# One instruction per head for the causal mask and the row maximum of the attention scores

## The chip, the cores and the metric

The kernel runs on one core of a Trainium2 chip. The metric is the device time of one execution in microseconds (us); less is better. A core has five engines with a queue of instructions each: TensorE (PE, matrix products; its weight loads are shown as PEld), VectorE (DVE), ScalarE (ACT), GpSimd (POOL) and SyncE (SP, which here only issues DMA transfers). An engine takes its instructions strictly in the order in which they were written, and waits on semaphores for the results of others. SBUF is the on-chip memory with 128 partitions; PSUM is the memory that TensorE writes to.

## The reference

Four sequences of 512 tokens with 1024 features go through causal attention with 32 heads (8 key and value heads, 32 features each), and then through a linear layer with a two-of-eight choice of low-rank additions. All is float32. What the change touches is this:

```python
scores = jnp.einsum('bhqd,bhkd->bhqk', q, k) / math.sqrt(HEAD_DIM)
scores = jnp.where(causal[None, None, :, :], scores, jnp.float32(-1e+20))
attn = jax.nn.softmax(scores, axis=-1)
out = jnp.einsum('bhqk,bhkd->bhqd', attn, v)
...
result = jnp.einsum('bsd,od->bso', x, base_w) + base_b
```

Around it stand layer norms, the projections for queries, keys and values, rotary embedding, the output projection, and the gate with its low-rank products.

## The kernel before

**Tiles.** The 2048 tokens are 16 tiles of 128 (`Tokens`, line 854). Tile `t` is number `i = t % 4` of its sequence, so that its queries meet `n = (i + 1) * 128` keys. The projections work on pairs of tiles in seven products of half blocks each, in place of eight (`seven`, line 724). Their bias is added when a product leaves PSUM: the lower half of the bias with the first product, and for the fourth the "bias step", which is the upper half less the lower half (`bias_step`, line 461; `bias_steps`, line 414). All four projections ("kv", "q", "o" and "f", the last one with `bbase_sb`) have a tile of their own for the step.

**Attention in groups.** The heads of a tile are done in groups (`Group`, line 1479). A group takes `n` heads of each of four quadrants (32 partitions each): 4 for `i` = 0, 2 for `i` = 1 and one for `i` = 2 and 3. That makes 2, 4, 8 and 8 groups for the four tiles of a sequence, 88 in all. `scores` (line 1490) has TensorE write the scores of all four quadrants into the only score tile `sc`, four PSUM banks, one for each quadrant. Then `softmax` (line 1552) runs on DVE in two parts of two quadrants each: line 1567 adds the triangular mask `cmask` to the last 128 columns of each row of scores, in place, and line 1577 takes the maximum of each whole row, negated, into `nmax`. For each quadrant, ACT computes exp(score + nmax) into `pr` and sums it (line 1519; with each goes a second instruction that reads the accumulator out), DVE takes the reciprocal of the sums (line 1548), and POOL multiplies (line 1533). TensorE transposes `pr` (line 1670), ACT or DVE copies the result out of PSUM (line 336 or 337, `prT<-pt_p`), and TensorE multiplies it with the values (line 1693). The next group's scores need the score tile free, that is all of this group's exponentials done.

**What sets the order.** No run-time scheduler: `Order` (line 92) plans the whole kernel when it is built. Every step on DVE, ACT, POOL and SP has a cost in us written into the code, and a rank ("urgent"; lower goes first); a step that may run on either of two engines, such as `copy` (line 332) and `combine` (line 340), goes to the one that is free sooner by these costs. TensorE's steps lie in lanes; the planner takes a step that is ready by its own clock, attention first and the dense projections into the gaps, and then prints all queues in that order. So a changed cost moves instructions in every queue. On the chip each queue keeps the printed order, whether or not the costs were right. The matmuls that use TensorE in parts of 32 rows or columns (scores and values) are planned next to each other, where that is possible (`PAIRED`, line 254); a step counts as safely ready when its inputs are `SAFE` = 0.3 us old by the plan (line 223).

Of the kernel before, what the change touches and what calls it, by code (L numbers as in the profile page):

```python
# [11 lines left out]
F32 = mybir.dt.float32  # L12
AF = mybir.ActivationFunctionType
ALU = mybir.AluOpType
AX = mybir.AxisListType

P = 128
# [5 lines left out]
MASKED = -1e30  # L23
QUADS = P // HD
# [67 lines left out]
class Order:  # L92
# [10 lines left out]
    def start(self, chain, at=0.0):  # L103
        task = Task()
        self._go_on(chain, task, at)
        return task
# [159 lines left out]
def kernel(  # L266
# [14 lines left out]
    nc = tc.nc  # L281
    NT, D = x.shape
    S = rope.shape[0]
# [12 lines left out]
    const = ctx.enter_context(tc.tile_pool(name="const", bufs=1))  # L296
# [20 lines left out]
    order = Order(banks)  # L317
    start = order.start

    def dve(us, urgent, issue):  # L320
        return Op(urgent, dve=(us, issue))

    def act(us, urgent, issue):
        return Op(urgent, act=(us, issue))

    def pool(us, urgent, issue):
        return Op(urgent, pool=(us, issue))
# [12 lines left out]
    def combine(urgent, out, in0, in1, op, engines=("dve", "pool"), n=512):  # L340
# [11 lines left out]

    ident = const.tile([P, P], F32, name="ident")
    make_identity(nc, ident)
    cmask = const.tile([P, P], F32, name="cmask")
    make_causal_mask(nc, cmask, MASKED)

    earlier = const.tile([P, E, E], F32, name="earlier")
# [2 lines left out]
        out=earlier,  # L361
# [15 lines left out]
    bbase_sb = const.tile([P, D], F32, name="bbase_sb")  # L377
# [9 lines left out]
    def loads(what):  # L387
# [13 lines left out]
    plain = {"kv": w_qkv[:, D:], "q": w_qkv[:, :D], "o": w_o, "f": w_base}  # L401

    width = {name: 256 if name == "kv" else 512 for name in plain}
# [8 lines left out]
        "f": bbase_sb,  # L412
    }
    bias_steps = {
        name: const.tile([P, width[name]], F32, name=f"bias_step_{name}") for name in plain
    }
    has_bias = {name: Task() for name in plain}

    def new_wide(name):
# [1070 lines left out]
    def scores(g):  # L1490

        tok, seq = g.tok, g.seq
        i, n = tok.i, (tok.i + 1) * P
        sc = ps_sc.tile([P, QUADS, 512], F32, tag="sc", name=f"sc_{g.name}")
        for c in range(g.n):
            for r in range(QUADS):
                rows = slice(r * HD, (r + 1) * HD)
                nc.tensor.matmul(  # L1498
                    sc[:, r, c * n : (c + 1) * n],
                    lhsT=tok.qT[g.kt][rows, (g.at + c) % GROUP, :],  # L1500
                    rhs=seq.kT[g.kt][rows, :n],
                    start=True,
                    stop=True,
                )
        sc4 = sc[:, :, : g.n * n].rearrange("p r (c k) -> p r c k", c=g.n)
        nmax = small.tile([P, QUADS, GROUP], F32, tag="nmax", bufs=3, name=f"nmax_{g.name}")
        total = small.tile([P, QUADS, GROUP], F32, tag="total", bufs=3, name=f"total_{g.name}")
        rtot = small.tile([P, QUADS, GROUP], F32, tag="rtot", bufs=3, name=f"rtot_{g.name}")

        def quadrant(r):  # L1510
            urgent = 1 + r / QUADS
            yield soft_slots.take()
            pr = soft.tile([P, GROUP, P], F32, tag="soft", name=f"pr_{g.name}_{r}")
            pr = g.pr[r] = pr.rearrange("p a b -> p (a b)")
            for c in range(g.n):
                yield act(
                    0.5 + n * 0.00079,
                    urgent,
                    lambda: nc.scalar.activation(  # L1519
                        pr[:, c * n : (c + 1) * n],  # L1520
                        sc4[:, r, c, :],
                        AF.Exp,
                        bias=nmax[:, r, c : c + 1],
                        accum_out=total[:, r, c : c + 1],
                    ),
                )
            g.exps[r].finish(order.at)
            yield g.rtot[r // 2]
            for c in range(g.n):
                yield pool(  # L1530
                    0.33 + n * 0.00089,
                    urgent,
                    lambda: nc.gpsimd.tensor_scalar(  # L1533
                        pr[:, c * n : (c + 1) * n],
                        pr[:, c * n : (c + 1) * n],
                        rtot[:, r, c : c + 1],
                        1.0,
                        ALU.mult,
                        ALU.mult,
                    ),  # L1540
                )
            g.normed[r].finish(order.at)

        def totals(h):
            some = slice(2 * h, 2 * h + 2)
            yield g.exps[some]
            yield dve(
                0.18, 1, lambda: nc.vector.reciprocal(rtot[:, some, : g.n], total[:, some, : g.n])  # L1548
            )
            g.rtot[h].finish(order.at)  # L1550

        def softmax():
            yield g.scored.done
            tok.q_left[g.kt] -= g.n
            if not tok.q_left[g.kt]:
                qT_slots.give(order.at)
            seq.left[g.kt] -= g.n
            if not seq.left[g.kt]:
                kT_slots.give(order.at)
            q = QUADS // g.parts  # L1560
            for r0 in range(0, QUADS, q):
                some = slice(r0, r0 + q)
                diag = sc4[:, some, :, i * P : n]
                yield dve(
                    0.15 + q * g.n * 0.135,
                    0,
                    lambda: nc.vector.tensor_tensor(  # L1567
                        out=diag,
                        in0=diag,
                        in1=cmask.unsqueeze(1).unsqueeze(1).to_broadcast([P, q, g.n, P]),  # L1570
                        op=ALU.add,
                    ),
                )
                yield dve(
                    0.15 + q * g.n * n * 0.00105,
                    0,
                    lambda: nc.vector.tensor_reduce(  # L1577
                        nmax[:, some, : g.n], sc4[:, some], AX.X, ALU.max, negate=True
                    ),
                )  # L1580
                for r in range(r0, r0 + q):
                    start(quadrant(r), order.at)

        start(softmax(), order.now)
        for h in range(QUADS // 2):
            start(totals(h), order.now)
# [192 lines left out]
    for tok in line:  # L1779
        n = min(GROUP, NQ // (tok.i + 1))  # L1780
# [5 lines left out]
    for k, g in enumerate(groups):  # L1786
# [6 lines left out]
        if k > 1:  # L1793
            needs += [s.done for s in groups[k - 2].turned]
        g.scored = Step(0.218 * blocks, partial(scores, g), needs, soon=soon)
        if tok.squares:
            g.scored.tiled = True
# [191 lines left out]
```

## Time and profile before

| what | value |
| --- | --- |
| time, median of 3 runs | 1162.27 us (1158.39 to 1164.69) |
| time of the profiled execution | 1156.95 us |
| its span, from first to last instruction | 1155.2 us |
| DVE busy | 842.5 us, 73% |
| ACT busy | 527.2 us, 46% |
| POOL busy | 636.6 us, 55% |
| DMA, bytes moved | 251.05 MB, mean 217 GB/s |
| granted TensorE clock over the span | 0.997 |

The rows of the profile read `line engine operation out<-in partitions x elements xcount | busy us, mean ns of one | idle time before, and who ended it`. A line is that of the kernel above, and of a helper where a helper issues the instruction. Busy time is a union, so that overlapping instructions are counted once. The time of an execution is about 1.75 us more than its span.

### The profile page before, as it was taken

How to read it: one execution, taken by the hardware profiler on the slowest of the kernel's cores; microseconds unless marked ns; L12 is line 12 of the kernel's file. 1: busy time of each engine (PE TensorE's matmuls, PEld its weight loads, DVE VectorE, ACT ScalarE, POOL GpSimd, SP SyncE). 2: the span in 40 equal slices, each digit the busy share in tenths (PEclk: the TensorE clock that was granted, in tenths of full speed). 3: DMA queues.
4: the chain of work that ended last, by engine and by line, in shares of the span. 5: the costliest groups of instructions: out<-in, count | busy, mean ns of one | idle time of the engine just before them, and what ended most of it. 6: DMA issues, size and time to landing. Idle time of an engine off the chain costs nothing.

```text
span 1155.2 us, 22058 instructions
## 1 busy us (share of the span) xinstructions
PE 1125.2 (97%) x7464; PEld 637.7 (55%) x7464; DVE 842.5 (73%) x1661; ACT 527.2 (46%) x1542; POOL 636.6 (55%) x875
## 2 busy tenths in 40 slices
PE   7999899999999999999999999999999999999997
PEld 3455555655446556665466455656754555556543
DVE  4778867878778876788778676688866787657564
ACT  0345555455435544465354245456453555454010
POOL 3676867763756644545665356464635564547231
PEclk9999999999999999999999999999999999999999
DMA  9777668656797458546696656754657744586682
GB/s 342 276 273 267 226 211 278 232 191 223 258 334 236 134 181 260 182 146 201 223 290 195 227 175 219 234 168 152 196 173 261 226 138 154 166 268 194 216 288 79
DMA packets 136239, 251.05 MB, mean 217 GB/s; under 512 B 14912, under 2 KB 30912, under 8 KB 136128
## 3 DMA queue, kind: packets, MB, share of 16 engines
q1 hardware_dynamic: 136128, 249.65, 65.3%
q8 instruction: 60, 0.98, 0.4%
q14 instruction: 51, 0.42, 0.1%
HBM read 225.87 MB, written 23.07 MB: 215 GB/s over the span
## 4 chain that ended last, share of the span: by engine, by line
PE 86%; DVE 7%; DMA 2%; POOL 2%; ACT 2%; issue 1%; SPq 0%; POOLq 0%; ACTq 0%; DVEq 0%
PE acc_f L646 19%; PE acc_o L646 16%; PE acc_q L646 13%; PE pt_p L1670 11%; PE acc_kv L646 8%; PE sc L1498 7%; PE av L1693 6%; PE acc_gl L646 2%; DVE nmax L1577 2%; PE pt_h L621 1%; PE pt_q L1121 1%; PE pt_xn L621 1%; ACT pr L1519 1%; POOL pr L1533 1%; DMA xa<-in_x_dram 1%
## 5 line engine op out<-in xcount | busy, mean ns | idle before, releaser
L1533 POOL TENSOR_SCALAR pr<-pr,rtot 128x256 f32<-128x256 f32 (+3 forms) x512 | 309.9, 620 | 220.6 <-DVE rtot L1548 158.2
L1519 ACT ACTIVATE pr<-sc,nmax 128x256 f32<-128x256 f32 (+3 forms) x512 | 264.1, 536 | 107.1 <-DVE nmax L1577 58.0
L1577 DVE TENSOR_REDUCE nmax<-sc 128x2 f32<-128x768 f32 (+3 forms) x176 | 198.2, 1126 | 32.0 <-ACT pr L1519 28.6
L336 ACT COPY prT<-pt_p 128x512 f32<-128x512 f32 (+1 forms) x260 | 132.8, 546 | 86.9 <-PE pt_p L1670 86.1
L1670 PE MATMUL pt_p<-ident,pr 128*128 128x128 f32 x1216 | 165.8, 276 | 2.2 <-DVE raw_k L1026 0.8
L1670 PEld LDWEIGHTS pt_p<-ident,pr 128*128 128x128 f32 x1216 | 137.9, 142 | 53.7 <-issue 39.9
L336 ACT COPY aT<-av 128x128 f32<-128x128 f32 (+2 forms) x82 | 25.1, 306 | 220.7 <-PE av L1693 202.0
L1567 DVE TENSOR_TENSOR sc<-sc,cmask 128x256 f32<-128x256 f32 (+2 forms) x176 | 96.5, 548 | 39.4 <-PE sc L1498 34.0
L646 PE MATMUL acc_f<-piece,s_f 128*128 128x512 f32 x256 | 118.7, 595 | 2.1 <-DVE s_f L344 2.1
L1519 ACT ACTIVATION_READ_ACCUMULATOR pr<-sc,nmax 128x1 f32 x512 | 109.0, 213 | 0.0
L646 PE MATMUL acc_o<-piece,aT 128*128 128x512 f32 x232 | 106.1, 594 | 0.0
L646 PE MATMUL acc_q<-piece,T_xn 128*128 128x512 f32 x224 | 105.2, 594 | 0.0
L646 PE MATMUL acc_o<-piece,s_o 128*128 128x512 f32 x224 | 103.2, 594 | 1.1 <-DMA piece<-in_w_qkv_dram 1.1
L1498 PE MATMUL sc<-kT,qT 32*128 32x384 f32 (+3 forms) x1024 | 94.3, 465 | 1.3 <-ACT pr L1519 1.3
L646 PE MATMUL acc_f<-piece,T_h 128*128 128x512 f32 x192 | 89.9, 594 | 0.1
L1693 PEld LDWEIGHTS av<-prT,v 128*32 128x32 f32 x2432 | 61.7, 109 | 49.0 <-issue 34.7
L344 POOL TENSOR_TENSOR y<-y,w 128x512 f32<-128x512 f32 x61 | 78.1, 1298 | 16.1 <-DVE w L590 8.6
L1693 PE MATMUL av<-prT,v 128*32 128x128 f32 x2432 | 84.9, 276 | 0.5 <-ACT T_xn L336 0.2
L646 PE MATMUL acc_kv<-piece,T_xn 128*128 128x512 f32 (+1 forms) x224 | 84.3, 511 | 0.8 <-DMA piece<-in_w_qkv_dram 0.8
L569 POOL TENSOR_TENSOR rstd<-veps,neg_half 128x1 f32<-128x1 f32 x64 | 36.3, 571 | 77.8 <-DVE veps L565 70.4
L646 PE MATMUL acc_q<-piece,s_q 128*128 128x512 f32 x160 | 75.2, 593 | 0.0
L646 PEld LDWEIGHTS acc_f<-piece,s_f 128*128 128x128 f32 x256 | 46.5, 190 | 51.8 <-issue 42.5
(178 smaller groups left out, 1544.9 us busy)
## 6 DMA issues: line engine op xcount, KB each, us to landing
piece<-in_w_qkv_dram SPq DMA_DIRECT2D x132, 256.0 KB, 3.8
piece<-mixed_f SPq DMA_DIRECT2D x128, 256.0 KB, 3.4
piece<-in_w_o_dram SPq DMA_DIRECT2D x116, 256.0 KB, 3.3
piece<-mixed_q SPq DMA_DIRECT2D x112, 256.0 KB, 3.5
piece<-mixed_o SPq DMA_DIRECT2D x112, 256.0 KB, 4.2
piece<-in_w_base_dram SPq DMA_DIRECT2D x96, 256.0 KB, 3.5
xa<-in_x_dram SPq DMA_DIRECT2D x32, 256.0 KB, 3.6
y<-in_x_dram SPq DMA_DIRECT2D x16, 512.0 KB, 5.2
```

What stands on the lines that cost most here:

```text
L336: act=(0.15 + n * 0.00085, lambda: nc.scalar.copy(out(), in_())),
L344: engine.tensor_tensor(out=out(), in0=in0(), in1=in1(), op=op)
L569: nc.gpsimd.tensor_tensor(out=self.rstd, in0=self.veps, in1=neg_half, op=ALU.pow)
L621: nc.tensor.transpose(pt[:, c, :], src()[:, at : at + P], ident)
L646: nc.tensor.matmul(acc[0][:, :n], lhsT=lhsT(c), rhs=w(c), start=(c == 0), stop=last)
L1498: nc.tensor.matmul(sc[:, r, c * n : (c + 1) * n], lhsT=tok.qT[g.kt][rows, (g.at + c) % GROUP, :], rhs=seq.kT[g.kt][rows, :n], start=True, ...
L1519: lambda: nc.scalar.activation(pr[:, c * n : (c + 1) * n], sc4[:, r, c, :], AF.Exp, bias=nmax[:, r, c : c + 1], accum_out=total[:, r, c : ...
L1533: lambda: nc.gpsimd.tensor_scalar(pr[:, c * n : (c + 1) * n], pr[:, c * n : (c + 1) * n], rtot[:, r, c : c + 1], 1.0, ALU.mult, ALU.mult,),
L1567: lambda: nc.vector.tensor_tensor(out=diag, in0=diag, in1=cmask.unsqueeze(1).unsqueeze(1).to_broadcast([P, q, g.n, P]), op=ALU.add,),
L1577: lambda: nc.vector.tensor_reduce(nmax[:, some, : g.n], sc4[:, some], AX.X, ALU.max, negate=True),
L1670: nc.tensor.transpose(pt[:, j, :], g.pr[r][:, j * P : (j + 1) * P], ident)
L1693: nc.tensor.matmul(av[r * HD : (r + 1) * HD, c, :], lhsT=g.seq.v[j][:, head * HD : (head + 1) * HD], rhs=g.prT[r][:, c * (i + 1) + j, :], ...
```

## The change

A wider mask tile holds 384 columns of zeros ahead of the triangle, so that its last `n` columns are the mask of a whole row of scores. For tiles with `i` > 0, the mask addition and the maximum become one DVE instruction for each head and quadrant, `tensor_tensor_reduce`: it writes -(score + mask) over the scores, and their minimum, which is the negated maximum, to `nmax`. ACT then computes exp(-x + nmax). The quadrants start in order, each when its own rows are done. Tiles with `i` = 0 keep the two instructions. The planner is given 0.17 + 0.00105 n us for the new instruction, without a term for the read of the accumulator.

The bias step of "f" is no longer a tile of its own: it is written over the upper half of `bbase_sb`, which nothing else reads.

```diff
-    cmask = const.tile([P, P], F32, name="cmask")
+    mask = const.tile([P, S], F32, name="mask")
+    nc.gpsimd.memset(mask[:, : S - P], 0.0)
+    cmask = mask[:, S - P :]
     make_causal_mask(nc, cmask, MASKED)
...
     bias_steps = {
-        name: const.tile([P, width[name]], F32, name=f"bias_step_{name}") for name in plain
+        name: const.tile([P, width[name]], F32, name=f"bias_step_{name}") for name in ("kv", "q", "o")
     }
+    bias_steps["f"] = bbase_sb[:, 512:]
...
+        def masked(r, c):
+            row = sc4[:, r, c, :]
+            nc.vector.tensor_tensor_reduce(
+                out=row,
+                in0=row,
+                in1=mask[:, S - n :],
+                scale=-1.0,
+                scalar=-MASKED,
+                op0=ALU.add,
+                op1=ALU.min,
+                accum_out=nmax[:, r, c : c + 1],
+            )
...
                         bias=nmax[:, r, c : c + 1],
+                        scale=-1.0 if i else 1.0,
                         accum_out=total[:, r, c : c + 1],
...
+            if i:
+                for r in range(QUADS):
+                    for c in range(g.n):
+                        yield dve(0.17 + n * 0.00105, 0, partial(masked, r, c))
+                    start(quadrant(r), order.at)
+                return
```

## The prediction

> **What bounds the kernel now.** I read the page's first part, then the busy times by stage, then PE's waits.
>
> ```profile
> PE 1125.2 (97%) x7464; PEld 637.7 (55%) x7464; DVE 842.5 (73%) x1661; ACT 527.2 (46%) x1542; POOL 636.6 (55%) x875
> ```
>
> TensorE is busy for 1125.2 of 1155.2 us, so 30.0 us are left in which it stands idle. The change works on DVE, which is busy 73%. Where do the 30 us lie? Stretches, with PE's busy time in the second place:
>
> ```profile
> 0.00:29.00 29.00, 21.12 (x57) 10.47 (x58) 12.66 (x26) 1.87 (x2) 8.85 (x20) 1.00 0.95 343
> 29.00:1100.00 1071.00, 1059.65 (x7289) 606.86 (x7288) 799.90 (x1577) 519.07 (x1531) 613.72 (x839) 1.00 0.66 216
> 1100.00:1155.20 55.20, 44.45 (x120) 20.41 (x118) 29.93 (x59) 6.30 (x9) 14.05 (x17) 0.97 0.51 180
> ```
>
> 7.88 us are lost at the start (the first 7.7 before any transpose can run) and 10.75 us at the end. In the 1071 us between, where the attention is, TensorE idles for 11.35 us. That is about all that a faster softmax can win. Who ended these waits:
>
> ```profile
> PE pt_xn L621 <- DVE xa L590: 7.9, 2, 7.7
> PE pt_q L1121 <- DVE raw_q L832: 3.6, 2, 2.6
> PE acc_f L646 <- DVE s_f L344: 2.1, 1, 2.1
> PE sc L1498 <- ACT pr L1519: 1.3, 1, 1.3
> ```
>
> Only one wait of 1.3 us is for the exponentials that the changed maximum feeds; the greatest after the start are for other work of DVE (`raw_q`, and `s_f` in the tail). The instruction orders of the two built programs agree in PE's last 75 rows and in DVE's and POOL's work beside them, so the tail stays, and so does the start.
>
> **What DVE gains.** Its rows, shapes kept apart:
>
> ```profile
> L1577 DVE TENSOR_REDUCE nmax<-sc 128x2 f32<-128x1024 f32 x64 | 78.2, 1222 | 9.8 <-ACT pr L1519 8.8
> L1577 DVE TENSOR_REDUCE nmax<-sc 128x2 f32<-128x768 f32 x64 | 61.3, 958 | 7.1 <-ACT pr L1519 5.5
> L1567 DVE TENSOR_TENSOR sc<-sc,cmask 128x256 f32<-128x256 f32 x128 | 54.7, 427 | 31.3 <-PE sc L1498 26.6 <-ACT pr L1519 3.0
> L1577 DVE TENSOR_REDUCE nmax<-sc 128x4 f32<-128x1024 f32 x32 | 39.1, 1222 | 6.9 <-ACT pr L1519 6.3
> L1567 DVE TENSOR_TENSOR sc<-sc,cmask 128x512 f32<-128x512 f32 x32 | 22.2, 694 | 6.9 <-PE sc L1498 6.5
> ...
> L337 DVE COPY prT<-pt_p 128x384 f32<-128x384 f32 x26 | 14.4, 556 | 8.7 <-PE pt_p L1670 8.0
> ...
> L344 DVE TENSOR_TENSOR s_f<-T_h,s_f 128x512 f32<-128x512 f32 x3 | 3.8, 1267 | 0.0
> ```
>
> Removed are the first five rows, 320 instructions: 78.2 + 61.3 + 54.7 + 39.1 + 22.2 = 255.5 us. Added are 384 rows of scores, 128 each of 256, 384 and 512 columns. No row shows the new instruction. The nearest is the mask addition, one source in PSUM and one in SBUF: 427 ns for 256 columns, 694 for 512; for 384 I take the 556 ns of the copy out of PSUM. 128 x (0.427 + 0.556 + 0.694) = 214.7 us. Each also has its accumulator read out by an instruction of its own. The trace shows one on DVE:
>
> ```profile
> 1125.15 0.17 DVE L1294 SCALAR_TENSOR_TENSOR w<-rank,ex 128x8 f32<-128x8 f32 x1
> 1125.25 0.08 DVE L1294 DVE_READ_ACCUMULATOR w<-rank,ex 128x1 f32 x1
> 1125.36 0.17 DVE L1298 RECIPROCAL gtot<-gtot 128x1 f32<-128x1 f32 x1
> ```
>
> It takes 81 ns in the median of 16, and begins while its main instruction still runs. 384 x 0.081 = 31.1 us, and the sum is 214.7 + 31.1 - 255.5 = **-9.7 us** of DVE work, the value I take. Cheap end: the read lies wholly beside its neighbours (in some of the 16 places the next instruction starts with it), -40.8 us. Dear end: it costs what ACT's read costs (213 ns, x512 in the page): 214.7 + 81.8 - 255.5 = +41.0. Dearer still, if two sources and an accumulator ran like the slow `s_f` row above, 1267 ns in place of 694 for 512 columns, or 1.12 ns more for each of 128 x 1152 = 147,456 columns: +165 us on top.
>
> [...] Here one source is in PSUM, and the mask addition's slope, (1226 - 427) / 768 = 1.04 ns a column up to 1024, is that of one source; but this row has no accumulator, and the only row with one has 8 columns. [...]
>
> DVE does not stay lighter. By the planner's cost the new instruction is cheap, so it hands DVE more of the shared steps: in the built order DVE's `prT` copies go from 50 to 70 (512 columns, 688 ns) and from 26 to 40 (384, 556 ns): +21.5 us for DVE, and ACT loses as many (-18.5 by its 588 and 481 ns). The other moves nearly cancel. So DVE ends about 12 us busier, at some 74%. ACT's 512 exponentials cost the same with a scale of -1 as with 1. One wider memset on POOL (128x128 takes 0.20 us, so some 0.4 us for 384 columns, an estimate) ends near 2.8 us, and POOL then idles until 6.16 us anyway. The bias step in place is the same single subtraction on POOL. Both cost nothing; if POOL had no idle there, the start would move by those 0.4 us.
>
> **What the softmax gains in latency.** For `i` = 3 the first exponential had to wait for 0.427 + 1.222 = 1.65 us of DVE; now for 0.694 + 0.081 = 0.78. The last maximum was there after 3.30 us, now after 4 x 0.775 = 3.10. ACT has 4 x (0.686 + 0.2) us to do meanwhile and so ends some 0.9 us sooner, in each of 80 groups. A group comes only every 1155 / 88 = 13.1 us, with dense matmuls between, so this latency is hidden already, as the wait of 1.3 us says. What is late next is the work that TensorE waits for now: `raw_q`, `raw_k`, `s_f`, pieces by DMA.
>
> **What TensorE pays.** The same 4560 matmuls in another order. Of the 88 score steps and 86 value steps, 74 stood as pairs; after, 65 or 66 do, and the stretches in the 32-row or 32-column form go from 100 to 108. Price of one, from PE's order of time:
>
> ```profile
> 867.54 1.88 PE L646 MATMUL acc_f<-piece,s_f 128*128 128x512 f32 x4
> 869.35 0.93 PE L1498 MATMUL sc<-kT,qT 32*128 32x384 f32 x8
> 870.21 1.08 PE L1693 MATMUL av<-prT,v 128*32 128x128 f32 x32
> ...
> 874.31 3.60 PE L646 MATMUL acc_f<-piece,T_h 128*128 128x512 f32 x8
> 877.84 0.93 PE L1498 MATMUL sc<-kT,qT 32*128 32x384 f32 x8
> ```
>
> Dense matmuls start every 0.429 us; 874.31 + 8 x 0.429 = 877.74, but the scores start at 877.84: 0.1 us to go over. A pair pays this on entry, between its halves and on the way out; split up, once more. 8 x 0.1 = +0.8 us.
>
> **The sum.** Span 1155.2 + 0.8 for the splits - 2.0 for waits in the middle = 1154.0. The 2.0 is chosen: the one softmax wait (1.3) and a little of the 11.35 idle, whose ends are 0 and 11.35 won, or as much again lost, since the new order puts new waits in place of the old. With the 1.75 us around the span, 1155.7 against 1156.95 in the profiled execution, 1.2 us less. That execution lies 0.5% under the median, so on the median's scale 1162.27 - 1.2 = **1161 us**.
>
> **The rivals.** A (my forecast, 0.45): TensorE bound before and after, 1156.5 to 1168 us, its own range. Within 0.5% of before, which is about what a measurement of this kernel can tell from no change.
>
> B (0.26), faster: exponentials 0.9 us sooner in 80 groups take away the waits of the middle. For it: they are ended mostly by DVE, whose queue also holds the maxima. Against it: few name the softmax. All 11.35 less 0.8: 1162.3 - 10.5 = 1152.
>
> C (0.20), slower: the plan's cost for the new instruction leaves out the read (0.708 planned for 512 columns, 0.775 by my rows), DVE carries 12 us more of copies, and each PE step planned with little to spare meets its operand late. It decides once `raw_q`, `s_f` or `prT` come more than the planned 0.3 us of slack late in many places. Priced at the idle of the middle again: 1162.3 + 11.35 + 0.8 = 1174.
>
> D (0.09), slower: the instruction doesn't do in one pass what it says. At the `s_f` row's rate a 512 row takes 1.267 + 0.081 = 1.35 us against 0.708 planned, so a group of `i` = 3 is 2.6 us late, of `i` = 2 2.0 and of `i` = 1 2.9: 32 x 2.6 + 32 x 2.0 + 16 x 2.9 = 194 us if all reached TensorE. A third, an estimate: 1226. It decides as soon as a 512 row takes over about 0.8 us.
>
> **The numbers.** Faster by over 0.5%: B and an edge of A, 0.30; slower: C and D, 0.29; within: 0.41. The range takes in A, B and C and leaves out D and the tails: 1147 to 1182. The cost of the read, from -40.8 to +41.0 us of DVE work, is inside it, as DVE has over 300 us idle.
>
> **What would show it.** Right: the new row at 0.42 to 0.72 us by width, reads near 80 ns, DVE at 72 to 75%, PE busy within a few us of 1125 and idle 8 to 15 us between 29 and 1100 us. A 512 row over 0.8 us speaks for D; PE waits on `prT`, `raw_q` or `sc` adding up to over 15 us for C; under 4 us of idle in the middle for B. I would be wrong altogether if PE's busy time itself fell or rose by over 10 us: then the ends that the profile models hide waits that I take for work.

## The result, and the profile after

| kernel | median us (lowest to highest) | ratio to before, 95% interval |
| --- | --- | --- |
| before, same chip | 1159.82 (1158.39 to 1164.69), 6 runs | |
| after | 1177.11 (1175.51 to 1178.39), 6 runs | 1.0144 (1.0127 to 1.0161) |

The change makes the kernel 1.4% slower, some 17 us. The forecast was 1161 us, 1.2 us less than the 1162.27 us that before had then; the time lies in the range, but on the wrong side of before. The profiled execution took 1175.51 us, its span is 1173.8 us: 18.6 us more than the span before.

The busy line of after:

```profile
PE 1131.7 (96%) x7464; PEld 638.5 (54%) x7464; DVE 849.6 (72%) x2146; ACT 518.7 (44%) x1503; POOL 636.5 (54%) x878
```

DVE is at 72%, no busier than the prediction had it. Where did 18.6 us come from? The stretches, cut in the same way (29 us of start, some 55 us of tail; PE's busy time in the second place):

```profile
0.00:29.00 29.00, 21.76 (x59) 10.67 (x60) 11.91 (x26) 1.87 (x2) 9.64 (x21) 1.00 0.96 348
29.00:1119.00 1090.00, 1065.91 (x7289) 607.61 (x7288) 808.11 (x2063) 510.56 (x1492) 612.81 (x841) 1.00 0.65 212
1119.00:1173.80 54.80, 43.99 (x119) 20.22 (x117) 29.54 (x58) 6.30 (x9) 14.06 (x17) 0.95 0.51 181
```

TensorE's idle time is 7.24 us at the start (before 7.88), 24.09 in the middle (before 11.35), 10.81 in the tail (before 10.75). So 12.7 us are new idle time in the middle, where the attention is, and PE's busy time grew by 6.5 us with the same 4560 matmuls (7464 records in the profile, two for each matmul but the transposes). Was that work? The matmuls' starts in the trace say no: summing, over all neighbours in PE's order, what a start comes later than the usual pitch of such a pair (delays over 40 ns only) gives 38.3 us before and 55.2 after, 16.9 more. (How the pairs are classed moves both sums, and their difference by a microsecond or two.) Nearly all of the loss is delay between matmuls, a part of it inside what the profile counts as busy.

The new instruction, shapes kept apart:

```profile
L1515 DVE CUSTOM_DVE_ANT_0 sc<-sc,mask 128x512 f32<-128x512 f32 x128 | 89.0, 695 | 30.6 <-ACT pr L1535 17.0 <-PE sc L1501 11.8
L1515 DVE CUSTOM_DVE_ANT_0 sc<-sc,mask 128x384 f32<-128x384 f32 x128 | 72.1, 563 | 43.1 <-ACT pr L1535 31.5 <-PE sc L1501 10.0
L1515 DVE CUSTOM_DVE_ANT_0 sc<-sc,mask 128x256 f32<-128x256 f32 x128 | 55.1, 431 | 40.1 <-ACT pr L1535 30.1 <-PE sc L1501 7.6
L1515 DVE DVE_READ_ACCUMULATOR2_ANT nmax<- 128x1 f32 x384 | 54.1, 141 | 0.0
```

Its price is as predicted: 695, 563 and 431 ns against 694, 556 and 427. The last column holds the news: the row stood idle for 113.8 us in all, and the greatest part was ended by ACT's exponentials (`pr`). The waits say it with counts (us in total, times, longest):

```profile
ACT pr L1535 <- DVE nmax L1515: 120.5, 155, 4.8
DVE sc L1515 <- ACT pr L1535: 78.6, 108, 1.5
PEld sc L1501 <- ACT pr L1535: 27.2, 28, 1.8
```

The first and the second together are a ping-pong: ACT waits for DVE's row, DVE waits for ACT's exponential. Before, the same pair was there in small:

```profile
ACT pr L1519 <- DVE nmax L1577: 58.0, 61, 2.0
DVE nmax L1577 <- ACT pr L1519: 28.6, 38, 1.4
```

One group of `i` = 2 in DVE's order of time (start, duration, and in brackets the idle time before and who ended it):

```profile
880.34 0.57 DVE L1515 CUSTOM_DVE_ANT_0 sc<-sc,mask 128x384 f32<-128x384 f32 x1 [0.20 <-PE sc L1501]
880.82 0.14 DVE L1515 DVE_READ_ACCUMULATOR2_ANT nmax<- 128x1 f32 x1
...
882.45 0.56 DVE L337 COPY prT<-pt_p 128x384 f32<-128x384 f32 x1 [0.83 <-PE pt_p L1693]
882.93 0.56 DVE L1515 CUSTOM_DVE_ANT_0 sc<-sc,mask 128x384 f32<-128x384 f32 x1
883.40 0.14 DVE L1515 DVE_READ_ACCUMULATOR2_ANT nmax<- 128x1 f32 x1
884.34 0.57 DVE L1515 CUSTOM_DVE_ANT_0 sc<-sc,mask 128x384 f32<-128x384 f32 x1 [0.80 <-ACT pr L1535]
884.83 0.14 DVE L1515 DVE_READ_ACCUMULATOR2_ANT nmax<- 128x1 f32 x1
```

and its exponentials on ACT:

```profile
883.64 0.58 ACT L1535 ACTIVATE pr<-sc,nmax 128x384 f32<-128x384 f32 x1 [0.38 <-DVE nmax L1515]
884.12 0.19 ACT L1535 ACTIVATION_READ_ACCUMULATOR pr<-sc,nmax 128x1 f32 x1
885.06 0.58 ACT L1535 ACTIVATE pr<-sc,nmax 128x384 f32<-128x384 f32 x1 [0.75 <-DVE nmax L1515]
```

The third row (882.93) is followed by the first quadrant's exponential, which starts at 883.64, when that third row's read is done; it needed only the first row, done at 880.96, and ACT, with copies until 883.26, stood idle for 0.38 us. The fourth row needs nothing of ACT at all. Yet it starts at 884.34, when that exponential has been read out, and the second exponential then waits for the fourth row. The reason is in the built program: its waits are kept for whole tiles. All four quadrants share the score tile `sc` and the tile `nmax`, so a row that writes one quadrant waits for the last exponential issued before it, of whatever quadrant, and an exponential waits for the last row issued before it. Counted in the built programs, 59 of before's softmax steps on DVE wait for an exponential in this way (48 maxima, 11 additions), and 141 of after's. The change cut two steps for each pair of quadrants into one for each row and issued the exponentials between them; so there are more places at which the two engines meet in one tile. What stands behind such a row on DVE (copies of `prT`, `raw_q`, `s_f`) waits with it. TensorE's list of waits shows the consequence:

```profile
PE sc L1501 <- ACT pr L1535: 7.1, 10, 1.5
PE pt_p L1693 <- POOL pr L1550: 3.8, 5, 1.5
PE pt_p L1693 <- ACT prT L336: 2.3, 3, 1.4
```

Before, the first of these was 1.3 us in one place.

### The profile page after: what moved, and what is told of

Its sections match the earlier page's. It is cut to its first block, busy times and chain, and to the rows that moved or that the text cites. A ratio compares the mean times of both kernels' runs of the same rounds, so it can differ in the third digit from the quotient of the medians.

```text
span 1173.8 us, 22474 instructions
## 1 busy us (share of the span) xinstructions
PE 1131.7 (96%) x7464; PEld 638.5 (54%) x7464; DVE 849.6 (72%) x2146; ACT 518.7 (44%) x1503; POOL 636.5 (54%) x878
## 4 chain that ended last, share of the span: by engine, by line
PE 71%; DVE 14%; ACT 5%; POOL 4%; issue 3%; DMA 2%; SPq 0%; ACTq 0%; POOLq 0%; DVEq 0%
PE acc_f L649 18%; PE acc_o L649 13%; PE acc_q L649 10%; PE pt_p L1693 9%; DVE sc L1515 6%; PE sc L1501 6%; PE av L1716 5%; PE acc_kv L649 5%; ACT pr L1535 5%; POOL pr L1550 2%; PE acc_gl L649 2%; DMA piece<-in_w_qkv_dram 2%; PE pt_q L1124 1%; PE pt_h L624 1%; DVE prT L337 1%
## 5 line engine op out<-in xcount | busy, mean ns | idle before, releaser
L1550 POOL TENSOR_SCALAR pr<-pr,rtot 128x256 f32<-128x256 f32 (+3 forms) x512 | 306.7, 614 | 269.1 <-DVE rtot L1565 207.1
L1535 ACT ACTIVATE pr<-sc,nmax 128x256 f32<-128x256 f32 (+3 forms) x512 | 266.1, 533 | 164.9 <-DVE nmax L1515 120.5
L1515 DVE CUSTOM_DVE_ANT_0 sc<-sc,mask 128x384 f32<-128x384 f32 (+2 forms) x384 | 216.2, 563 | 113.8 <-ACT pr L1535 78.6
L336 ACT COPY prT<-pt_p 128x512 f32<-128x512 f32 (+1 forms) x226 | 116.5, 545 | 58.8 <-PE pt_p L1693 56.6
L1535 ACT ACTIVATION_READ_ACCUMULATOR pr<-sc,nmax 128x1 f32 x512 | 105.4, 206 | 0.0
L344 POOL TENSOR_TENSOR y<-y,w 128x512 f32<-128x512 f32 x61 | 81.2, 1347 | 15.3 <-DMA piece<-in_w_base_dram 7.0
L337 DVE COPY prT<-pt_p 128x512 f32<-128x512 f32 (+1 forms) x110 | 70.1, 639 | 24.2 <-PE pt_p L1693 23.6
L1501 PEld LDWEIGHTS sc<-kT,qT 32*128 32x128 f32 x1024 | 39.5, 184 | 65.9 <-issue 29.0
```

Of the source, the lines that this page charges most:

```text
L336: act=(0.15 + n * 0.00085, lambda: nc.scalar.copy(out(), in_())),
L337: dve=(0.15 + n * 0.00105, lambda: nc.vector.tensor_copy(out(), in_())),
L344: engine.tensor_tensor(out=out(), in0=in0(), in1=in1(), op=op)
L1501: nc.tensor.matmul(sc[:, r, c * n : (c + 1) * n], lhsT=tok.qT[g.kt][rows, (g.at + c) % GROUP, :], rhs=seq.kT[g.kt][rows, :n], start=True, ...
L1515: nc.vector.tensor_tensor_reduce(out=row, in0=row, in1=mask[:, S - n :], scale=-1.0, scalar=-MASKED, op0=ALU.add, op1=ALU.min, accum_out=n ...
L1535: lambda: nc.scalar.activation(pr[:, c * n : (c + 1) * n], sc4[:, r, c, :], AF.Exp, bias=nmax[:, r, c : c + 1], scale=-1.0 if i else 1.0, ...
```

## The experiments

The **theory**: the waits through the shared score tile make the loss; the instruction itself costs and wins next to nothing. The first **rival** is the prediction's case C (the plan's costs are too low, DVE gets too many copies, operands come late); others are the order of the steps by itself, the bias step, and the tile of the maxima in place of the score tile. Tiles can be split without moving anything: the planner doesn't know these waits, and prints the same queues. In the table, "waits" are the softmax steps on DVE that wait for an exponential in the built program. Each row has runs of before on its own chip beside it, so rows are best compared by the ratio.

| kernel | order of | tiles | waits | median us | ratio to before (interval) |
| --- | --- | --- | --- | --- | --- |
| halves | after | by two quadrants | 31 | 1152.9 | 0.9945 (0.9927 to 0.9962) |
| quads | after | by quadrant | 4 | 1152.06 | 0.9945 (0.9921 to 0.9969) |
| quads_stats | after | by quadrant, sums by half | 4 | 1153.76 | 0.9941 (0.9918 to 0.9964) |
| nmax_quads | after | only the maxima's by quadrant | 141 | 1177.55 | 1.0148 (1.0116 to 1.0179) |
| fused_old_order | before | whole | 54 | 1158.8 | 0.9988 (0.9971 to 1.0004) |
| fused_old_quads | before | by quadrant | 4 | 1153.43 | 0.9947 (0.9931 to 0.9963) |
| before_halves | before, two instructions | by two quadrants | 2 | 1155.76 | 0.9967 (0.995 to 0.9984) |
| before_quads | before, two instructions | by quadrant | 4 | 1150.22 | 0.9913 (0.989 to 0.9935) |
| before_quarters | own, two instructions | whole | 231 | 1227.91 | 1.058 (1.0556 to 1.0603) |
| bias_alone | before, two instructions | whole | 59 | 1160.48 | 1.0011 (0.9991 to 1.0031) |
| after_cost | own, planned cost 0.26 | whole | 160 | 1174.65 | 1.0128 (1.0097 to 1.0159) |
| after_cost_quads | as after_cost | by quadrant | 4 | 1160.56 | 1.0006 (0.9994 to 1.0018) |
| rows_first | own, rows ahead of exponentials | whole | 12 | 1177.02 | 1.0153 (1.0126 to 1.018) |
| rows_first_quads | as rows_first | by quadrant | 4 | 1174.4 | 1.0128 (1.0102 to 1.0153) |
| rows_first_quads_cost | own, planned cost 0.26 | by quadrant | 4 | 1196.4 | 1.0324 (1.03 to 1.0348) |

### The tiles split, nothing moved

`halves` gives the scores and the maxima a tile for every two quadrants, every instruction and every queue as in after; `quads` one for each quadrant (`i` = 0's few steps and the copies `aT<-av`, which share the space, are then issued quadrant by quadrant). Of the edit of `quads`:

```diff
-        sc = ps_sc.tile([P, QUADS, 512], F32, tag="sc", name=f"sc_{g.name}")
+        sc = [ps_sc.tile([P, 512], F32, tag=f"sc{r}", name=f"sc{r}_{g.name}") for r in range(QUADS)]
...
-                    sc[:, r, c * n : (c + 1) * n],
+                    sc[r][:, c * n : (c + 1) * n],
```

> The changed kernel with score and maximum tiles for two quadrants each; instructions and order of every queue are those of the changed kernel. 31 fused rows still wait for an exponential. Theory W: most of the way, 1156 to 1168. Rival O: 1172 to 1178, as with a tile for each quadrant.

> The changed kernel with a score tile and a maximum tile for each quadrant in place of one for all four; every queue keeps the order of the changed kernel (for tiles with i = 0 the mask addition and the maximum are issued for each quadrant). Of the fused rows, 4 in place of 131 or so then wait for an exponential of ACT. Theory W (rows of one score tile wait for each other's exponentials, and the DVE queue stands still behind them): the 78.6 us of DVE idle time ended by ACT fall under 10, TensorE's idle time between 29 us and the tail falls from 24 to under 14, and the time falls by at least 12 us, to 1153 to 1165. Rival O (the new order itself, with its split pairs and its copies moved to DVE, makes TensorE wait): at most 4 us less than 1177, 1172 to 1178.

Measured: 1152.9 and 1152.06 us, 24 to 25 us less than after, and less than before too. The middle of `halves`, and then of `quads`:

```profile
29.00:1097.00 1068.00, 1059.63 (x7290) 608.62 (x7289) 806.97 (x2063) 502.44 (x1492) 607.28 (x841) 1.00 0.66 217
29.00:1097.00 1068.00, 1061.22 (x7293) 609.57 (x7293) 796.24 (x2097) 499.14 (x1494) 606.69 (x841) 1.00 0.66 217
```

PE idles there for 8.4 and 6.8 us in place of 24.1. Of the two waits of the ping-pong, ACT's was 120.5 us in 155 places and DVE's 78.6 in 108. In `halves` they are down to

```profile
ACT pr L1541 <- DVE nmax L1521: 40.0, 50, 5.1
DVE sc L1521 <- ACT pr L1541: 15.3, 26, 0.9
```

In `quads` DVE's is gone from the list, and ACT's is

```profile
ACT pr L1538 <- DVE nmax L1518: 18.2, 23, 4.4
```

The delays between matmuls, summed as above, fall from 55.2 to 34.0 us in `quads`, and PE's busy time from 1131.7 to 1126.7 (`halves`: 1125.1): what had looked like more work was delay. `halves` says most, as not one instruction differs from after, nor its place; only the tiles do, and with them the waits.

`quads_stats` splits the sums and their reciprocals as well:

> The changed kernel with tiles for each quadrant, and the sums and their reciprocals also in a tile for each half; order as in the changed kernel. If waits between the halves through these two small tiles still cost: 1145 to 1151. If TensorE has nothing left to win but its own work: 1150 to 1154, as with the quadrant tiles alone.

1153.76 us: nothing more is to be had there.

`nmax_quads` splits the maxima's tile alone:

> The changed kernel with the maxima's tile alone split by quadrant and the score tile left whole; all queues as in the changed kernel. 131 fused rows still wait for an exponential of another quadrant through the score tile. If the score tile is what ties them: 1174 to 1180 us, as the changed kernel. If the maxima's tile were the tie: 1150 to 1160 us.

1177.55 us, as after. The score tile by itself ties the engines, and the small tile adds nothing to that. Whether the maxima's tile, left whole beside split score tiles, would tie them as well no run shows: `halves` and `quads` split both.

### The tiles split in the kernel before

The same edit on before, with its two instructions in its order (by quadrant each addition and each maximum becomes one for every quadrant, twice as many as in before; by halves no instruction changes):

> The kernel before with score and maximum tiles for two quadrants each; order and instructions as before. Its second maximum of a group waited for the exponentials of the first half (28.6 us of DVE idle time, 38 times). Theory W: these go, and the time falls a little, 1152 to 1159 against 1160. Rival O: nothing to gain here, 1158 to 1162.

> The kernel before with a score and a maximum tile for each quadrant; PE's order as before, mask additions and maxima issued for each quadrant. Separates what the fused instruction gives from what the tiles give. Theory W with a small gain by the fusion: 1153 to 1158, above the 1152 of the changed kernel with the same tiles. If the tiles are all: 1150 to 1153.

1155.76 and 1150.22 us. The second is the fastest kernel of this study, 0.9% faster than before, without the change. In its list of waits DVE's is gone, and ACT's is down from 58.0 us in 61 places to

```profile
ACT pr L1522 <- DVE nmax L1578: 11.5, 6, 4.5
```

So before paid for the shared tile too, through its 59 waits.

### More waits without the fused instruction

`before_quarters` does the mask addition and the maximum quadrant by quadrant:

```diff
-            self.parts = 2
+            self.parts = 4 if tok.i else 2
```

> The kernel before, with mask addition and maximum of tiles with i > 0 done quadrant by quadrant (four parts in place of two), still as two instructions; 231 of these steps wait for ACT, against 59. Theory W: the slowdown comes without any fused instruction, 1168 to 1190. Rival F (the slowdown needs the fused instruction and its accumulator read): 1158 to 1166, for some 26 us more of DVE work in an engine that has 300 us idle.

1227.91 us, with the two old instructions. The same pair of waits has grown, and now DVE's addition waits as well (3.0 us in 7 places in before):

```profile
ACT pr L1519 <- DVE nmax L1577: 104.0, 130, 1.4
DVE nmax L1577 <- ACT pr L1519: 94.2, 125, 1.5
...
DVE sc L1567 <- ACT pr L1519: 49.0, 79, 1.0
```

So a finer split over one shared tile goes with a loss, and with more waits, without the fused instruction too. (Its plan also differs and it has more instructions, DVE 891.3 us busy; no run splits its tiles, so how much of the 68 us is waits isn't shown.)

### The fused instruction alone

`fused_old_order` puts a part's fused rows where its maximum stood and drops its addition; the plan and all other steps stay as before:

> The fused instruction in the order of before: the planner sees the two steps of before with their costs; the first issues nothing, the second issues the fused rows of its two quadrants. PE, ACT and SP have the order of before. Theory W: 45 rows wait for an exponential, as 48 maxima did before, so about the time of before, 1155 to 1164. Rival O: also the time of before, 1157 to 1163. A third theory, that the fused instruction with its read is too slow by itself: 1168 or more.

1158.8 us, no difference that can be told. `fused_old_quads` does so with tiles by quadrant:

> The fused rows in the order of the kernel before, with score and maxima tiles by quadrant: the same queues as the fastest kernel so far (two instructions, tiles by quadrant, 1150.2 us), only that the fused rows stand where the maximum of two quadrants stood and the mask additions are gone. Says what the fused instruction is worth by itself with no wait for tiles on either side. Theory: PE is the bound and DVE's 10 to 20 us of work hide, 1148 to 1154 us. Rival: the quicker first exponential shortens something once the false waits are gone, 1140 to 1147 us.

1153.43 us; the two instructions with the same tiles and order, `before_quads`, gave 1150.22 (their intervals just touch). In the traces DVE is busy for 807.4 us in the first and 848.4 in the second (some 6 us of that come from the finer split; before has 842.5). **41 us less work on DVE buy nothing**: TensorE, busy 97 to 98% of both, is the bound.

### The other half of the change

`bias_alone` has only the bias step in place:

> The kernel before with the other half of the change alone: the f bias step kept in the upper half of the bias's own tile. Every queue has the same instructions in the same order. Theory of the shared score tile: the bias has no part in the loss, 1160 us within 0.4% of the kernel before. Rival: if part of the 17 us comes from the bias step (a read of the bias tile that now waits for the step's write), the time rises, by up to a few us.

1160.48 us: no part of the loss that can be told.

### The plan's costs

`after_cost` tells the planner what a row and its read take by the trace:

```diff
-                        yield dve(0.17 + n * 0.00105, 0, partial(masked, r, c))
+                        yield dve(0.26 + n * 0.00105, 0, partial(masked, r, c))
```

> The changed kernel with the planner's cost of a fused row raised from 0.17 to 0.26 us beside its part by length, which is the row and its 0.14 us read as the trace times them; one score tile as in the changed kernel. Rival C as the prediction put it (the plan doesn't count the read, so DVE is given too many copies): the loss goes, 1158 to 1165 us. Theory of the shared score tile: 160 of the softmax steps on DVE still wait for exponentials, against 141, and the plan knows no wait: 1172 to 1183 us.

> The changed kernel with the higher planned cost of a fused row (1174.7 us with one tile), now with tiles by quadrant and the same order of its queues except for the steps of the unmasked first block. A second order in which the tiles alone change. Shared score tile: 1150 to 1160 us. If that order is slow by itself, as the order with all rows first turned out to be: 1165 to 1176 us.

1174.65 and 1160.56 us. The true cost doesn't repair the loss; splitting the tiles takes 14 us off this order as well (the theory's range was missed by half a microsecond). That this order is still 0.6% behind `quads`, some 8 us, shows what two plans that differ in one cost can differ by on their own.

### All rows ahead of the exponentials

If a row's waits come from exponentials issued before it, issuing all rows of a group first takes them away, with one tile as before:

```diff
                         yield dve(0.17 + n * 0.00105, 0, partial(masked, r, c))
+                for r in range(QUADS):
                     start(quadrant(r), order.at)
```

> The changed kernel with one score tile as before, but the exponentials of a group are started in the plan only after all its fused rows, so that 12 steps in place of 141 on scores and maxima wait for ACT. The first exponential starts some 2.3 us later than the changed kernel plans it. Theory W (the waits between rows of one tile): faster than the changed kernel by 10 us or more, 1152 to 1167. Rival L (an early first exponential is what matters): no faster than the changed kernel, 1175 or more.

1177.02 us: the theory missed here. The fused rows' waits for ACT are gone (of the softmax steps on DVE only the maxima of `i` = 0 still wait for ACT in the list, 8.7 us), and the kernel is as slow as after. Two more runs ask why:

> The kernel with all fused rows of a group ahead of its exponentials (1177 us), now with score and maxima tiles by quadrant; the order of its queues stays, except for the steps of the unmasked first block. In the one-tile version an exponential waits for the last fused row issued before it, 3.1 us after the scores; with tiles by quadrant it waits for its own row alone, 0.8 us. If the one-tile version was slow by that wait: 1150 to 1162 us. If it was slow by its order (exponentials put later by the plan, operands due at other times): 1170 to 1178 us.

> All fused rows of a group ahead of its exponentials, tiles by quadrant, and the planned cost of a fused row raised from 0.17 to 0.26 us beside its part by length, so that the plan comes out different. The trace of the version with the lower cost has two gaps of 4 to 6 us in which PE waits for raw_q and s_o, which stand behind eight fused rows and other work on DVE. If these were an accident of one plan, or come from rows planned too short: 1150 to 1163 us. If putting the exponentials after all rows makes operands late in any plan: 1168 to 1180 us.

1174.4 and 1196.4 us, the second above both of its ranges. With tiles by quadrant an exponential waits for its own row alone, and next to nothing is won; with another cost in the plan the loss more than doubles. So it is the order that this edit makes, and no tile. In `rows_first_quads` two long gaps stand out among TensorE's waits:

```profile
PE acc_o L649 <- DVE s_o L344: 5.5, 1, 5.5
PE pt_p L1700 <- DVE raw_q L776: 4.1, 1, 4.1
```

In the second, `raw_q` leaves PSUM on DVE at 372.17 us, behind eight fused rows in a block, 368.60 to 372.31; PE stands from 368.8 on. In the first, what stands ahead of `s_o` on DVE isn't fused rows, but the two old instructions of a tile with `i` = 0 and its transposes. Why the planner comes to such orders when exponentials start late wasn't followed further, nor whether all of the 22 to 44 us over `quads` lie in such gaps. That stays open. It is a second way to lose the same time, and not the one that after goes, which `halves` undoes without moving a step.

## Why the prediction was wrong

- **The failed step** is "What the softmax gains in latency", and with it the term of the sum that came from it, "- 2.0 for waits in the middle". Measured there are 12.7 us more of idle time (24.1 for 11.35), and the 6.5 us more of busy time are for the most part delay too. The step had the last maximum there "after 4 x 0.775 = 3.10" us and ACT done "some 0.9 us sooner", as if the rows ran one after the other. They don't: a row waits for an exponential of another quadrant through the shared tile, and the exponential for a row. In the group shown above, of `i` = 2, for which the same reckoning gives 4 x (0.556 + 0.081) = 2.55 us, the rows take from 880.34 to about 884.97 us, 4.6 us: 0.80 of that is the wait for the exponential, and some 1.4 a copy of `prT`, with its own wait, between the second row and the third. The prediction asked what stands behind each moved step, but not what the smaller steps wait for. The trace of before held the clue, 38 places where `nmax` waits for `pr`, a wait that no data need explain; and the fused row adds the write to `sc` that the maximum didn't have.
- "**this latency is hidden already**" was read off one wait of 1.3 us. With 141 waits through the tile PE idles for 24.1 us in the middle, and even before's 59 weren't hidden: `before_quads` is 0.9% faster.
- **Rival C** had the sign and nearly the size (1174 us) by the wrong mechanism. It priced the idle of the middle once more, 11.35 us (measured 12.7), but for plan costs and copies. `quads` has the same plan and the same copies and runs in 1152; `after_cost` has the read in the plan and runs in 1174.65. Its sign to look for, PE's waits on `prT`, `raw_q` and `sc` adding up to over 15 us, was just met (7.1 for `sc`, 7.3 for `prT` and 0.8 for `raw_q`, 15.2 in all; some 5.6 before) and would have been taken as proof. The same symptom has several causes.
- **B** ("exponentials 0.9 us sooner in 80 groups take away the waits of the middle", 1152 us) is the time that comes out once the tile is split: 6.8 us of idle, 1152.06. But the two old instructions with the same tiles come to 1150.22, so it isn't the new instruction's sooner exponentials that bring it, and that the times agree is luck.
- **D** is refuted: 695 ns for 512 columns, not 1.267 us. With an accumulator and with one source in PSUM, the row's slope is (695 - 431) / 256 = 1.03 ns a column; in before the copy has (688 - 556) / 128 = 1.03, the mask addition 1.04.
- **DVE's work**: the read is mis-sized, 141 ns and not 81, but it begins before its row has ended and the next row starts beside it (in `quads`, 863.21 us for both), so it costs the queue little. In the same plan (`fused_old_order` against before) DVE's busy time falls by 842.5 - 825.8 = 16.7 us, where -9.7 was predicted, within the bounds. After the planner's 34 more copies (50 to 70 and 26 to 40, as read from the order) after is 7.1 us above before, where +12 was said.
- **Start and tail** came out as said (7.24 us idle against 7.88, and 10.81 against 10.75). The 0.8 us for the splits stands in no run by itself; `halves`, with after's order on TensorE, is faster than before, so they can't cost much.
- **The last warning**, that busy time which rises means hidden waits, was right in kind: +6.5 us with the same matmuls, gone in `quads` (1126.7), though it set 10 us as the bound.

## What to carry to other kernels

Before one step over a shared tile is cut into several that another engine is to follow, ask for each new piece whom it waits for in the built program, and not only what data it needs: waits are kept by tile, so the tile must be cut along the same lines as the steps. A wait in the old profile that no data explain (a maximum waiting for exponentials) is worth following before anything is made cheaper; here cutting the tile alone won 0.9%, and 41 us less work on an engine that isn't the bound won nothing. And a loss of the forecast size doesn't prove the forecast mechanism: the run that keeps every instruction in its place and takes away one wait does.

## What the runs showed of the hardware

- The accumulator read behind the fused row takes 141 ns in the profile of after (x384), behind the scalar-tensor-tensor row 81 ns in that of before (x16). In the places shown both begin before their main instruction ends: 880.82 against 880.91 us, and 1125.25 against 1125.32.
- ACT's exponentials cost the same to within 8 ns with a scale of -1 as with 1, as the prediction had it: 687, 582 and 474 ns for 512, 384 and 256 columns in after, 686, 586 and 482 in before.
- One long gap cost TensorE more than its length. After the 5.50 us that `rows_first_quads` waits for `s_o`, eight dense records take 5.74 us, 0.72 each in place of 0.43 (0.429 in before):

```profile
584.54 5.74 PE L649 MATMUL acc_o<-piece,s_o 128*128 128x512 f32 x8 [5.50 <-DVE s_o L344]
```

By stretches of 1 us the granted clock there is 1.00 up to 581 us, 0.93 from 581 to 582, 0.50 from 582 to 588, 0.66 from 588 to 589, and 1.00 after that (0.84 over 575 to 585 as a whole, 0.69 over 585 to 591). So it fell some 2.8 us after TensorE's last work (579.04) and was full again some 4.1 us after the gap's end. After the gap of 4.11 us, which ends at 372.91, the clock fell only when TensorE was at work again: it is 1.00 up to 373, 0.82 from 373 to 374, 0.50 up to 377 and 0.97 from 377 to 378 (0.98 over 300 to 400 as a whole). Reckoned from these figures as time at 0.50, an estimate, that is 6.8 us the first time and 3.4 the second. What sets these times no run shows.

- The clock was down without a long gap too, and so it can have a small part in after's loss. Between 140 and 152 us, where none of after's gaps is over 1.5 us but TensorE is busy for only 2.40 us of the first 5, its granted clock is 0.57 (0.50 in each us from 141 to 150); before has 0.66 from 140 to 145 and 1.00 from 145 to 152. Reckoned in the same way that is some 10.3 us at half clock against 3.4, worth at most 3.4 of the 18.6 us (an estimate from these clocks).
